# Batches of 3, 3 and 2 steps in the attention of an image network's first layer

## The chip, the cores and the metric

The kernel runs on one core of a Trainium2 chip, everything in fp32. The metric is the device time of one execution in microseconds (us). The kernel before takes 3935.89 us, the median of three runs (3935.14 to 3937.17).

## What is computed

Eight images of 512 channels and 32 x 32 positions go through four layers: attention with eight heads and three inner steps (layer 0), attention with one head of 512 channels (layer 1), an upsampling, leaky ReLU and downsampling (layer 2), and convolutions with mixed experts (layer 3). The change lies in layer 0, which is, cut to what matters:

```python
h = group_norm(x, gn_scale, gn_bias)
q, k, v = split(einsum('oc,bchw->bohw', qkv_w, h) + qkv_b)      # 8 heads of 64 channels
attn = softmax(einsum('bnsd,bntd->bnst', q, k) * 64 ** -0.5, axis=-1)   # 1024 x 1024 a head
h = einsum('bnst,bntd->bnsd', attn, v)
for _ in range(3):                                              # inner steps
    h = h + 0.1 * tanh(h @ inl_w.T + inl_b)
x = x + (proj_w @ h + proj_b)
```

## The kernel before, in words

`tile_sequence` works image by image: layer 0, layer 1, layer 2, and at the end layer 3 for all images. A second copy of the program, which subtracts row maxima before the exponentials, follows behind a condition and is not taken with these inputs.

In layer 0 the projections q, k and v of an image come first (`product`, L384: a matrix product in seven smaller ones, whose matmuls stand at L414). Then comes the attention of the image, the part that changes. It has eight **groups** (L596), one for each of four pairs of heads and each half of the 1024 queries, and each group has eight **steps**, one for each 128 keys: 64 steps an image, 512 in all.

- `scores(t)` (L599) makes one step's scores: two matmuls (L266), one for each head of the pair, each with a contraction over 64 rows, side by side in the array, into the two banks of one PSUM tile of pool `ps_sc`. ScalarE takes the exponential of both banks in one instruction (L612) into a buffer `e` of SBUF. VectorE adds `e` to the running sum of the group (L616, L618).
- `weighted(t)` (L620) multiplies the exponentials with the values (L627): two matmuls of 64 columns each, into one bank of pool `ps_mm` that gathers all eight steps of the group.
- `normalised(g)` (L632) ends a group: two matmuls with ones make the totals over the keys (L637) in a bank of pool `ps_tp`; VectorE takes their reciprocal (L641) and multiplies the gathered values with it into `hf` (L642); GpSimd adds the sums and the reciprocal to a guard that is looked at once at the end (L644).

A matmul of the program is two matmul instructions in the profile.

[...]`ps_sc` two tiles of two banks, `ps_tp` two banks, `ps_mm` two banks. Each pool hands out its buffers in turn, and a tile can be written once the tile that had the buffer before has been read. The exponentials have five buffers in turn (`tmp`, L77), the running sums two (L80).

The loop (L647) sets the order of TensorE: two steps of scores, then the values of the two steps before them, and so on. `normalised(g)` follows in the batch that holds steps 2 and 3 of the next group. The order of instructions is finally set by the framework's own scheduler, which may move an instruction ahead of others of its engine; in the attention it leaves TensorE in the order of the loop.

After the groups come the inner steps. The first one (L657 to L662) may begin before the last group is done: its first two products (P1 and C11 of `product`, written to `inl_A`) need only the first half of the positions. Their two banks are one of `ps_mm` and one of `ps_tp` (L661). The next product needs sums and differences of the four quarters of `hf` (`quarter_sums`, L365, with its subtractions at L378 to L381).

## Time and profile before

| what | us | share or count |
| --- | --- | --- |
| span of the profiled execution | 3934.4 | 37957 instructions |
| TensorE matmuls busy | 3868.2 | 98% |
| TensorE weight loads busy | 2032.6 | 52%, beside matmuls |
| VectorE busy | 2593.8 | 66% |
| ScalarE busy | 1105.0 | 28% |
| GpSimd busy | 436.1 | 11% |
| scores, L266, on the chain that ended last | | 13% of the span |
| values, L627, on the same chain | | 11% of the span |
| totals, L637 | 66.2 | 256 instructions |
| one image's attention, TensorE busy, from 564 to 691 us | 125.86 of 127.00 | 536 instructions |

An engine that is busy 98% of the span does not tell by itself that it sets the time; the chain of work that ended last, followed back from the end, does: 90% of it is TensorE. A group's line gives its count, the busy time of all its instructions together and the mean of one; the matmuls of a pair run side by side, so that the mean (616 ns for scores) is more than busy time over count. Behind the bar stands the idle time of the engine just before these instructions, and what ended it. In a timeline, equal instructions that follow each other are one row: its start, its length and their number.

### The profile page before, as it was taken

What the parts mean: (1) busy time and instruction counts of PE and PEld (TensorE: products, weight loads), DVE (VectorE), ACT (ScalarE), POOL (GpSimd) and SP (SyncE); (2) the same over time, 40 slices, a digit from 0 to 9 for tenths busy, and PEclk for the clock granted to TensorE, in tenths of its full rate; (3) what the DMA queues carried; (4) which work ended last, traced back from release to release, by engine and by line L of the source; (5) the groups of instructions that cost most, each with busy time, mean ns of one, the idle gap of its engine ahead of it and who ended that gap; (6) DMA issues with size and microseconds to landing.
All of it is one profiled execution on the core that took longest, in us unless ns stands there. A gap on an engine that the chain in (4) does not pass through costs nothing.

```text
span 3934.4 us, 37957 instructions
## 1 busy us (share of the span) xinstructions
PE 3868.2 (98%) x14630; PEld 2032.6 (52%) x14630; DVE 2593.8 (66%) x3690; ACT 1105.0 (28%) x1507; POOL 436.1 (11%) x310
## 2 busy tenths in 40 slices
PE   8999999999999999999999999999999999999998
PEld 4336653476435763366434754357534764346543
DVE  4777848764686647775586646765487655766786
ACT  1421224212332114212241123322142122421333
POOL 5310003000120003100030002200031001301000
PEclk9999999999999999999999999999999999999999
DMA  5002310122101310023101221013200131003432
GB/s 197 19 0 83 115 57 1 40 77 100 38 0 59 118 68 11 0 83 115 56 1 59 79 81 37 1 70 107 78 1 24 60 115 57 1 0 112 164 134 103
DMA packets 85792, 247.86 MB, mean 63 GB/s; under 512 B 10480, under 2 KB 33024, under 8 KB 78816
## 3 DMA queue, kind: packets, MB, share of 16 engines
q1 hardware_dynamic: 69712, 220.23, 15.8%
q10 hardware_dynamic: 13824, 12.59, 1.0%
q0 software_dynamic: 2064, 12.51, 0.8%
q8 instruction: 117, 1.92, 0.2%
q14 instruction: 75, 0.61, 0.0%
HBM read 185.40 MB, written 59.90 MB: 62 GB/s over the span
## 4 chain that ended last, share of the span: by engine, by line
PE 90%; DVE 7%; issue 1%; DMA 1%; ACT 1%; SPq 0%; DVEq 0%; ACTq 0%
PE scores L266 13%; PE av L627 11%; PE inl_X L414 6%; PE dn L941 6%; PE up L920 5%; PE v_X L414 4%; PE inl_Y L414 4%; PE av_X L854 4%; PE c L1150 3%; PE v_Y L414 3%; PE av_A L854 3%; PE v_A L414 3%; PE inl_A L414 3%; PE av_Y L854 2%; PE proj_X L414 2%; PE q_X L414 2%
## 5 line engine op out<-in xcount | busy, mean ns | idle before, releaser
L612 ACT ACTIVATE e<-scores 128x1024 f32<-128x1024 f32 x512 | 497.1, 1021 | 632.7 <-PE scores L266 632.0
L618 DVE TENSOR_TENSOR acc<-acc,e 128x1024 f32<-128x1024 f32 x384 | 494.1, 1287 | 122.7 <-ACT e L612 101.6
L266 PE MATMUL scores<-q,k 64*128 64x512 f32 x2048 | 511.0, 616 | 7.0 <-ACT e L612 3.6
L627 PE MATMUL av<-e,v 128*64 128x512 f32 x2048 | 494.1, 604 | 0.0
L644 POOL TENSOR_TENSOR seen<-seen,acc 128x512 f32<-128x512 f32 x128 | 212.3, 1659 | 1574.9 <-DVE acc L618 1569.9
L266 PEld LDWEIGHTS scores<-q,k 64*128 64x128 f32 x2048 | 175.7, 186 | 334.3 <-ACT e L612 163.2
L627 PEld LDWEIGHTS av<-e,v 128*64 128x64 f32 x2048 | 124.8, 136 | 338.8 <-issue 335.8
L941 PEld LDWEIGHTS dn<-dn_op,up 128*128 128x128 f32 (+1 forms) x2048 | 239.9, 192 | 46.3 <-issue 24.3
L904 DVE SCALAR_TENSOR_TENSOR up<-up,leak 128x512 f32<-128x512 f32 (+1 forms) x264 | 174.9, 687 | 132.9 <-ACT leak L903 124.9
L941 PE MATMUL dn<-dn_op,up 128*128 128x126 f32 (+5 forms) x2048 | 244.7, 275 | 10.1 <-DVE up L904 9.5
L903 ACT ACTIVATE leak<-up 128x512 f32<-128x512 f32 (+1 forms) x264 | 150.0, 595 | 248.9 <-DVE up L904 125.4
L641 DVE RECIPROCAL inv<-total 128x512 f32<-128x512 f32 x64 | 214.7, 3354 | 0.0
L920 PE MATMUL up<-halo,up_op 126*128 126x512 f32 (+1 forms) x384 | 182.8, 605 | 0.4 <-DVE up L904 0.3
L414 PE MATMUL inl_X<-T_hf,w_inl 128*128 128x512 f32 x384 | 172.6, 592 | 0.0
L644 POOL TENSOR_TENSOR seen<-seen,inv 128x512 f32<-128x512 f32 x64 | 125.1, 1955 | 417.6 <-DVE inv L641 417.6
L414 PE MATMUL inl_A<-hf,w_inl 128*128 128x512 f32 x384 | 169.5, 594 | 0.0
L616 DVE TENSOR_TENSOR acc<-e,e 128x1024 f32<-128x1024 f32 x64 | 85.0, 1329 | 102.4 <-ACT e L612 100.7
L508 ACT ACTIVATE inl_U<-inl_U,inl_b 128x512 f32<-128x512 f32 x96 | 64.0, 714 | 304.7 <-DVE inl_U L523 304.7
L519 DVE TENSOR_TENSOR inl_U<-inl_X,inl_P 128x512 f32<-128x512 f32 x96 | 61.8, 685 | 116.0 <-PE inl_X L414 116.0
L736 POOL TENSOR_TENSOR seen<-seen,acc 128x512 f32<-128x512 f32 x16 | 22.6, 1410 | 1019.9 <-DVE acc L728 1019.9
L1150 PE MATMUL c<-rim,mixed 128*128 128x512 f32 x288 | 124.9, 592 | 0.0
L414 PEld LDWEIGHTS inl_A<-hf,w_inl 128*128 128x128 f32 x384 | 72.3, 190 | 94.5 <-issue 88.8
(302 smaller groups left out, 5757.6 us busy)
## 6 DMA issues: line engine op xcount, KB each, us to landing
halo<-ypad_u SPq DMA_DIRECT2D x128, 252.0 KB
halo<-ypad_u SPq DMA_DIRECT2D x128, 198.0 KB
w_v<-stored_u_v SPq DMA_DIRECT2D x14, 1792.0 KB
x<-in_x_dram SPq DMA_DIRECT2D x32, 512.0 KB
spill_u<-z SPq DMA_DIRECT2D x28, 512.0 KB
z<-spill_u SPq DMA_DIRECT2D x28, 512.0 KB
out_dram<-z SPq DMA_DIRECT2D x28, 512.0 KB
w_q<-stored_u_q SPq DMA_DIRECT2D x7, 1792.0 KB
```

The lines of the kernel that those rows point to most:

```text
L266: nc.tensor.matmul(ps[r], k[r], q[r], start=True, stop=(shift is None))
L414: nc.tensor.matmul(dst, lhs, rhs, start=(opens and s == 0 and cc == 0), stop=(cc == 1 and s == rows), skip_group_check=True,)
L612: nc.scalar.activation(e, ps, AF.Exp, scale=HD ** -0.5)
L618: nc.vector.tensor_add(accs[g], accs[g], e)
L627: nc.tensor.matmul(avs[g][rows[r]], v[:, jc, ts(2 * oc + r, HD)], e[:, ts(r, HALF)], start=(jc == 0), stop=(jc == SC - 1),)
L641: nc.vector.reciprocal(inv, ps)
L644: nc.gpsimd.tensor_add(seen, seen, part)
L854: nc.tensor.matmul(ps[:, ts(s, QR)], left[:, j, at : at + P], right[:, j, :], start=(what in ("P1", "U2", "W") and s == 0 and j == 0), sto ...
L904: nc.vector.scalar_tensor_tensor(dst, ps, SQRT2, t, ALU.mult, ALU.max)
L920: nc.tensor.matmul(ps[i], op[0 : IR * n, :], halo.tile(t)[0 : IR * n, c + i, :], start=True, stop=True,)
L941: nc.tensor.matmul(rows[:, r0 - first : r1 + 1 - first, c0 : c1 + 1], up[t][0:k, c, ts(cc, P)], op[:, r0 - 4 * t + 3 : r1 + 4 - 4 * t, c0 ...
L1150: nc.tensor.matmul(banks[g].rearrange("p (h w) -> p h w", w=W), wt[:, at : at + P], h1[:, ky + 16 * g : ky + 16 * g + 16, kx : kx + W], st ...
```

## The change

Scores and values alternate in batches of three, three and two steps, so that a group has three batches instead of four. The first and second batches have three score steps that are all made before the values of the batch before. For the third one `ps_sc` has no buffer, so steps 2 and 5 of a group get two single banks of `ps_tp` instead, and two exponentials of 512 columns in place of one of 1024. Six steps' exponentials may be alive at once, so the buffers of exponentials become six. `normalised(g)` follows in the third batch of the next group, that is behind the values of its steps 3, 4 and 5; for the last group it follows at the end, as before. The purpose is that TensorE switches less often between the 64-row tiles of the scores and the 64-column tiles of the values.

```diff
         if n == HALF:
             return work.tile([P, n], F32, tag="half", name=name, bufs=2)
-        return work.tile([P, n], F32, tag="tmp", name=name, bufs=5)
+        return work.tile([P, n], F32, tag="tmp", name=name, bufs=6)
...
         def scores(t):
             g, jc = divmod(t, SC)
             oc, sh = groups[g]
-            ps = ps_sc.tile([P, S], F32, tag="scores", name=f"scores_{b}_{t}")
+            apart = jc in (2, 5)
+            if apart:
+                ps = [bank(ps_tp, f"scores_{b}_{t}_{r}") for r in range(2)]
+            else:
+                pair = ps_sc.tile([P, S], F32, tag="scores", name=f"scores_{b}_{t}")
+                ps = [pair[:, ts(r, HALF)] for r in range(2)]
             scores_T(
-                [ps[:, ts(r, HALF)] for r in range(2)],
+                ps,
...
             e = tmp(f"e_{b}_{t}", S)
-            nc.scalar.activation(e, ps, AF.Exp, scale=HD ** -0.5)
+            if apart:
+                for r in range(2):
+                    nc.scalar.activation(e[:, ts(r, HALF)], ps[r], AF.Exp, scale=HD ** -0.5)
+            else:
+                nc.scalar.activation(e, pair, AF.Exp, scale=HD ** -0.5)
...
-        n = len(groups) * SC
-        for t in range(0, n + 4, 2):
-            for u in (t, t + 1):
-                if u < n:
-                    scores(u)
-            for u in (t - 2, t - 1):
-                if 0 <= u < n:
-                    weighted(u)
-            if t >= SC + 2 and (t - 2) % SC == 0:
-                normalised((t - 2) // SC - 1)
+        batches = [
+            range(g * SC + i, g * SC + j)
+            for g in range(len(groups)) for i, j in ((0, 3), (3, 6), (6, 8))
+        ]
+        for i in range(len(batches) + 1):
+            for t in batches[i] if i < len(batches) else ():
+                scores(t)
+            for t in batches[i - 1] if i else ():
+                weighted(t)
+
+            g, part = divmod(i, 3)
+            if g and (part == 2 or i == len(batches)):
+                normalised(g - 1)
```

## The prediction, made before the changed kernel had run

> **What bounds the kernel now.** I read the page first: the busy shares, the chain that ended last, and the costliest groups.

> ```profile
> PE 3868.2 (98%) x14630; PEld 2032.6 (52%) x14630; DVE 2593.8 (66%) x3690; ACT 1105.0 (28%) x1507; POOL 436.1 (11%) x310
> ...
> PE 90%; DVE 7%; issue 1%; DMA 1%; ACT 1%; SPq 0%; DVEq 0%; ACTq 0%
> ...
> L612 ACT ACTIVATE e<-scores 128x1024 f32<-128x1024 f32 x512 | 497.1, 1021 | 632.7 <-PE scores L266 632.0
> L618 DVE TENSOR_TENSOR acc<-acc,e 128x1024 f32<-128x1024 f32 x384 | 494.1, 1287 | 122.7 <-ACT e L612 101.6
> L266 PE MATMUL scores<-q,k 64*128 64x512 f32 x2048 | 511.0, 616 | 7.0 <-ACT e L612 3.6
> L627 PE MATMUL av<-e,v 128*64 128x512 f32 x2048 | 494.1, 604 | 0.0
> ...
> L641 DVE RECIPROCAL inv<-total 128x512 f32<-128x512 f32 x64 | 214.7, 3354 | 0.0
> ```

> TensorE sets the time, and attention is 511.0 + 494.1 us of it. ScalarE waits for TensorE (632.0 us), while TensorE waits for ScalarE 3.6 us in the whole run. So only two things can move the time: what TensorE itself spends in attention, or a new wait on it. Next the timeline inside one attention (image 1; start, length, engine):

> ```profile
> 577.39 1.94 PE L627 MATMUL av<-e,v 128*64 128x512 f32 x8
> 579.26 1.99 PE L266 MATMUL scores<-q,k 64*128 64x512 f32 x8
> 581.18 1.94 PE L627 MATMUL av<-e,v 128*64 128x512 f32 x8
> 582.94 1.03 PE L637 MATMUL total<-acc,ones 128*64 128x512 f32 x4
> 583.90 1.99 PE L266 MATMUL scores<-q,k 64*128 64x512 f32 x8
> 584.02 3.36 DVE L641 RECIPROCAL inv<-total 128x512 f32<-128x512 f32 x1
> 587.52 2.06 POOL L644 TENSOR_TENSOR seen<-seen,inv 128x512 f32<-128x512 f32 x1 [8.21 <-DVE inv L641]
> ```

> Here: TensorE alternates without a gap. A block of two score steps starts 1.92 us before the values (579.26 to 581.18), a block of two value steps 1.87 us before the scores (577.39 to 579.26). The reciprocal begins 1.08 us after the totals begin, runs 3.36 us, and nothing on TensorE waits for it. Last, the timelines of the start and the end of the same attention:

> ```profile
> 560.48 1.13 PE L266 MATMUL scores<-q,k 64*128 64x512 f32 x4
> 562.03 1.13 PE L266 MATMUL scores<-q,k 64*128 64x512 f32 x4 [0.41 <-DVE v L495]
> 564.06 2.04 PE L266 MATMUL scores<-q,k 64*128 64x512 f32 x8 [0.91 <-ACT e L612]
> 566.04 1.94 PE L627 MATMUL av<-e,v 128*64 128x512 f32 x8
> ```

> ```profile
> 683.68 1.99 PE L266 MATMUL scores<-q,k 64*128 64x512 f32 x8
> 685.59 3.65 PE L627 MATMUL av<-e,v 128*64 128x512 f32 x16
> 690.32 1.08 PE L637 MATMUL total<-acc,ones 128*64 128x512 f32 x4 [1.07 <-DVE acc L618]
> 691.33 7.13 PE L414 MATMUL inl_A<-hf,w_inl 128*128 128x512 f32 x16
> 694.14 3.35 DVE L641 RECIPROCAL inv<-total 128x512 f32<-128x512 f32 x1
> 699.51 2.84 PE L414 MATMUL inl_X<-v,w_inl 128*128 128x512 f32 x6 [0.18 <-DVE v L379]
> ```

> At the start TensorE idles 0.41 + 0.91 us. At the end it idles 1.07 us for the last running sum, and then the inner step's first product (inl_A, 7.13 us) covers the last reciprocal.

> [...] Scores run in 64-row tiles, values and totals in 64-column tiles. [...] so a score matmul that waits for a bank holds everything behind it. The totals' wait above is such a case. [...] A third pair of scores therefore needs two more banks, and the change takes the only two that `ps_tp` has.

> **The change, part by part.**

> *Fewer switches.* Sixteen value matmuls take 3.65 us and eight take 1.94, so two steps stream in 1.71 us; for scores x8 less x4 gives 0.86 us a step. A block of two score steps costs 1.92 - 1.72 = 0.20 us over streaming, a block of two value steps 1.87 - 1.71 = 0.16. One alternation costs 0.35 us. A group of 8 steps has 4 alternations now and 3 after: 64 groups x 0.35 = **-22.4 us**. Totals follow values in the same tiling and cost the same as before.

> *The two half exponentials for steps 2 and 5.* The trace of layer 1 has such halves at 0.5 us apiece, so a step takes 1.03 instead of 1.02 us of ScalarE, which waits for TensorE anyway: 0. *The sixth buffer.* Three steps in work and three being made are 6; the exponential of step t waits for the addition of step t-6, which is done at least a block before: 0.

> *Totals two batches later, in the same pool as steps 2 and 5.* This is the added wait. `ps_tp` hands out two banks in turn. A group now takes five: step 2's pair, step 5's pair, the total. The next pair takes the other bank first and the total's own bank second, and that one is free only when the reciprocal has read it. The built order of instructions says so: the second matmul of step 2 of the next group waits for VectorE, at the count of that reciprocal; its first matmul waits for nothing. Queued behind it on TensorE are two value steps, and everything else. With the totals starting at 0: the score block starts at 0.96 (583.90 - 582.94); its third step would start at 0.96 + 0.10 (half of the block's switch cost) + 2 x 0.86 = 2.78. The reciprocal starts at 1.08, if VectorE is free, and ends at 1.08 + 3.36 = 4.44. VectorE is free: the addition of the last exponential, made before three value steps and the totals, ends about 0.8 us before. A release takes 0.06 us (the last addition ended 690.26, the totals that waited for it began 690.32), and weights not loaded ahead cost 0.05 to 0.10 us. So the matmul runs at 4.60 instead of 2.78: a stall of 1.82 us. It comes after groups 0 to 5 of an image; total 6 is followed by values, total 7 by the inner step. 6 x 8 images = 48 stalls x 1.82 = **+87.4 us**. Bounds: 1.55 (weights loaded ahead, an early release) to 2.0 (an addition still running before the reciprocal): 74 to 96 us.

> *The start.* Steps 0 to 5 come before the first values. Step 2 has banks at once and fills the 0.91 us idle; steps 3, 4 and 5 then follow the exponentials of 0, 1 and 2, at 1.02 us each, slower than streaming. I put the first values at about 567.1 with six steps done, against 566.04 with four; two steps are worth 1.72, so -0.65 us an image: **-5 us** (-2 to -8).

> *The end.* Total 6 now comes just before total 7 and its reciprocal just before the last. The inner step's first product writes into a bank that the sixth group's values held, freed only by that group's multiplication, which the order puts behind both reciprocals (about 13.0 us after the start of the last score block). The order meets this by doing the other bank's half first, both its products. Counted from that score block: totals 7 end at 8.0, the first half waits for reciprocal 6 until 9.0, its second product about 0.9 for a copy, the other half starts at 13.5 and finds its bank free. The waiting product of the sums starts at 18.0; before, it started at 699.51 - 683.68 = 15.83, with a value step and a total (1.72 us) less to do. So 18.0 - 17.55 = +0.5 us an image: **+4 us** (0 to +10). The 1.07 us that total 7 waits for now is in this.

> Sum: -22.4 + 87.4 - 5 + 4 = +64 us; 3935.9 + 64 = 4000 us.

> **Rivals.** *The wait is hidden* (7%): were the bank free earlier than the count of the reciprocal says, the switches alone would show: 3935.9 - 22.4 - 5 + 4 = 3912 us, faster. The order of instructions speaks against it; for it only that the wait is not in the trace of before, so that its length is worked out and not seen. *The pair is torn wholly apart* (5%): if the first matmul of the waiting pair is held as well and the two then run one after the other, each stall grows by one matmul, 0.86 us: 48 x 0.86 = 41, 4041 us. The score pairs start within 0.01 us of each other in the trace, so they do depend on issue order. *The end goes wrong* (5%): VectorE's three subtractions took up to 1.75 us beside GpSimd in the trace of before, 0.68 alone; if the four that stand behind the last multiplication all take that, the product of the sums slips by some 4 us an image: +32, 4032 us. *VectorE becomes the bound* (1%): it has 7 x 1.29 + 3.36 + 0.68 = 13.1 us of work in a group of 15.6 to 17.5 us.

> **How the numbers follow.** The likeliest case (82%) gives 4000 us. Its unknown terms, 74 to 96 for the stalls, -2 to -8 and 0 to +10 at the ends, span 3980 to 4020. Below lies the hidden wait, above the other two. A result within 0.2% of no change would need the stalls to come to just 23 us: 1%. Faster 7%, slower 92%.

> **What would show it.** In the profile after: groups of 15.65 us become 17.5 (totals to totals, 16.00 now); a line in which scores wait some 1.8 us, 48 times, for the reciprocal; alternations of 0.35 us, three in a group; the reciprocal still 1.08 us behind its totals. It would be wrong if scores wait for nothing or for ScalarE, or if the reciprocal starts late.

## The result, and the profile after

| | us, median | from | to |
| --- | --- | --- | --- |
| before | 3936.53 | 3935.14 | 3940.61 |
| after | 4006.66 | 4004.24 | 4008.63 |

The changed kernel takes 1.0176 times as long (95% interval 1.0159 to 1.0194): 70 us more, where 64 were forecast. The page of the changed kernel, busy times, the engines of the chain that ended last, and the costliest groups:

```profile
PE 3905.6 (97%) x14630; PEld 2062.1 (51%) x14630; DVE 2660.6 (66%) x3690; ACT 1109.9 (28%) x1635; POOL 425.6 (11%) x310
...
PE 91%; DVE 7%; DMA 1%; ACT 1%; issue 0%; SPq 0%; POOL 0%; ACTq 0%; POOLq 0%; DVEq 0%
...
L627 DVE TENSOR_TENSOR acc<-acc,e 128x1024 f32<-128x1024 f32 x384 | 537.1, 1399 | 121.3 <-ACT e L621 93.2
L266 PE MATMUL scores<-q,k 64*128 64x512 f32 x2048 | 548.5, 612 | 37.0 <-DVE inv L650 33.2
...
L636 PE MATMUL av<-e,v 128*64 128x512 f32 x2048 | 481.4, 601 | 0.0
...
L650 DVE RECIPROCAL inv<-total 128x512 f32<-128x512 f32 x64 | 213.7, 3350 | 46.6 <-PE total L646 46.6
...
L619 ACT ACTIVATE e<-scores 128x512 f32<-128x512 f32 x256 | 145.7, 610 | 52.1 <-PE scores L266 52.1
```

TensorE still sets the time, and ScalarE still waits for it. The new thing stands behind the bar of the scores' line (L266): 33.2 us of idle time that the reciprocal ended. The scores are also busy 37.5 us longer (511.0 before), though their 2048 matmuls are the same; the values (L636) are busy 12.7 us less (494.1 before). The waits of TensorE (engine line, engine line waited for, us in total, times, longest us) count the new ones:

```profile
PE scores L266 <- DVE inv L650: 33.2, 48, 0.7
...
PE inl_A L414 <- DVE inv L650: 7.1, 8, 0.9
PE inl_A L414 <- ACT inl_P L514: 5.4, 8, 0.7
```

There are 48 waits of scores for the reciprocal, as many as forecast, but at 0.69 us each and not at 1.8. The timeline of one group, from its totals on, tells why; its columns are start, length, engine, line:

```profile
598.01 1.03 PE L646 MATMUL total<-acc,ones 128*64 128x512 f32 x4
...
598.97 2.84 PE L266 MATMUL scores<-q,k 64*128 64x512 f32 x10
599.09 3.36 DVE L650 RECIPROCAL inv<-total 128x512 f32<-128x512 f32 x1 [0.83 <-PE total L646]
...
602.50 1.12 PE L266 MATMUL scores<-q,k 64*128 64x512 f32 x2 [0.69 <-DVE inv L650]
...
603.55 1.94 PE L636 MATMUL av<-e,v 128*64 128x512 f32 x8
...
615.46 1.03 PE L646 MATMUL total<-acc,ones 128*64 128x512 f32 x4
```

The score block has twelve matmul instructions, and ten of them run from 598.97. Eight belong to steps 0 and 1, two to the waiting pair: its first matmul has its bank, and both its instructions run alone, at 2.78 and 3.21 us after the totals began. Its second one needs the bank of the total. The reciprocal starts 1.08 us after the totals (599.09 - 598.01) and ends at 4.44; the last two instructions run from 4.49, and the values behind them on TensorE from 5.54. So TensorE counts as busy while only one of the two halves of the array works, and is wholly idle for 0.69 us only. What the wait costs is read from the period, from totals to totals. It is 17.45 us after each of the groups 0 to 5 of an image (here 615.46 - 598.01). Before it was 16.00: in the trace before, the totals at 582.94 are followed by these.

```profile
598.94 1.03 PE L637 MATMUL total<-acc,ones 128*64 128x512 f32 x4
```

With one alternation less the period would be 15.65, as two experiments below confirm. So the stall is 17.45 - 15.65 = **1.80 us**, and 48 of them are 86 us.

The end of the same attention:

```profile
698.19 1.99 PE L266 MATMUL scores<-q,k 64*128 64x512 f32 x8
...
702.73 1.03 PE L646 MATMUL total<-acc,ones 128*64 128x512 f32 x4
...
703.59 1.89 PE L636 MATMUL av<-e,v 128*64 128x512 f32 x8
...
703.81 6.57 DVE L650 RECIPROCAL inv<-total 128x512 f32<-128x512 f32 x2 [0.83 <-PE total L646]
...
705.31 1.03 PE L646 MATMUL total<-acc,ones 128*64 128x512 f32 x4
...
707.22 1.98 PE L414 MATMUL inl_A<-hf,w_inl 128*128 128x512 f32 x4 [0.89 <-DVE inv L650]
...
716.08 2.74 PE L414 MATMUL inl_X<-v,w_inl 128*128 128x512 f32 x6
```

The waiting product of the sums starts 716.08 - 698.19 = 17.89 us after the last score block. Before it was 15.83, with 1.72 us less to do: +0.34 us an image.

Added up over the attention of an image, from the first matmul of its q to the first one of `inl_Y` in both traces, the change costs 7.69 and 7.52 us in the first two images and 8.18 to 8.20 in the six others: **64.4 us** together. The two profiled spans differ by 71.4 us (4005.8 and 3934.4). The other 7 lie outside the attention, above all in layer 2, where stretches of the trace after show TensorE at half its clock. The table by window of one of them (us of the window, PE, PEld, DVE, ACT and POOL busy, granted clock as a share of full speed, share of the DMA engines, GB/s):

```profile
2300.00:2304.00 4.00, 2.44 (x18) 1.87 (x16) 0.90 (x3) 0.79 (x2) 0.00 (x0) 1.00 0.69 218
2304.20:2311.00 6.80, 6.41 (x30) 6.42 (x31) 1.62 (x3) 1.31 (x4) 0.00 (x0) 0.50 0.79 254
2311.00:2316.00 5.00, 5.00 (x47) 5.00 (x46) 0.00 (x0) 0.98 (x2) 0.00 (x0) 1.00 0.87 281
```

The clock falls to 0.50 after TensorE waited in the stretch before, and 6.8 us later it is back. All such stretches together are 34.5 us after and 21.3 before, and TensorE is busy in 20.15 and 9.30 us of them. With half of that put down as lost, an estimate from the granted 0.50, it is 10.1 against 4.7, some 5.4 us. The change does not bring this wait with it. The same one stands in the trace before, where no half clock follows:

```profile
2260.00:2264.00 4.00, 2.18 (x17) 1.83 (x15) 1.33 (x3) 1.09 (x2) 0.00 (x0) 1.00 0.74 234
2264.00:2268.00 4.00, 3.90 (x35) 3.90 (x35) 1.34 (x3) 1.62 (x3) 0.00 (x0) 1.00 0.77 245
```

The last section sets the two side by side. How much of the 5.4 us the timed runs lost too is open. The unchanged kernel itself varies so: in 36 further runs of it the mean granted clock lay between 0.995 and 0.998 and the time between 3949 and 3935 us. The run of it that was profiled, at 0.998, was among those with the least half clock.

### The profile page after: what moved, and what is told of

It is laid out like the page before. It is cut to its first block, busy times and chain, and to the rows that moved or that the text cites. A ratio compares the mean times of both kernels' runs of the same rounds, so it can differ in the third digit from the quotient of the medians.

```text
span 4005.8 us, 37999 instructions
## 1 busy us (share of the span) xinstructions
PE 3905.6 (97%) x14630; PEld 2062.1 (51%) x14630; DVE 2660.6 (66%) x3690; ACT 1109.9 (28%) x1635; POOL 425.6 (11%) x310
## 3 DMA queue, kind: packets, MB, share of 16 engines
q8 instruction: 117, 1.92, 0.2%
## 4 chain that ended last, share of the span: by engine, by line
PE 91%; DVE 7%; DMA 1%; ACT 1%; issue 0%; SPq 0%; POOL 0%; ACTq 0%; POOLq 0%; DVEq 0%
PE av L636 11%; PE scores L266 11%; PE inl_X L414 6%; PE dn L954 6%; DVE inv L650 5%; PE up L933 5%; PE v_X L414 4%; PE inl_A L414 4%; PE inl_Y L414 4%; PE av_X L867 4%; PE c L1163 3%; PE v_Y L414 3%; PE av_A L867 3%; PE v_A L414 3%; PE av_Y L867 2%; PE proj_X L414 2%
## 5 line engine op out<-in xcount | busy, mean ns | idle before, releaser
L627 DVE TENSOR_TENSOR acc<-acc,e 128x1024 f32<-128x1024 f32 x384 | 537.1, 1399 | 121.3 <-ACT e L621 93.2
L266 PE MATMUL scores<-q,k 64*128 64x512 f32 x2048 | 548.5, 612 | 37.0 <-DVE inv L650 33.2
L621 ACT ACTIVATE e<-scores 128x1024 f32<-128x1024 f32 x384 | 372.8, 1024 | 480.7 <-PE scores L266 480.6
L636 PE MATMUL av<-e,v 128*64 128x512 f32 x2048 | 481.4, 601 | 0.0
L266 PEld LDWEIGHTS scores<-q,k 64*128 64x128 f32 x2048 | 195.4, 186 | 383.2 <-issue 280.2
L653 POOL TENSOR_TENSOR seen<-seen,acc 128x512 f32<-128x512 f32 x128 | 245.3, 1916 | 1356.5 <-DVE acc L627 1347.1
L636 PEld LDWEIGHTS av<-e,v 128*64 128x64 f32 x2048 | 130.6, 136 | 326.8 <-issue 307.8
L414 PE MATMUL inl_A<-hf,w_inl 128*128 128x512 f32 x384 | 173.7, 598 | 12.5 <-DVE inv L650 7.1
L414 PE MATMUL inl_X<-T_hf,w_inl 128*128 128x512 f32 x384 | 172.6, 592 | 0.0
L619 ACT ACTIVATE e<-scores 128x512 f32<-128x512 f32 x256 | 145.7, 610 | 52.1 <-PE scores L266 52.1
L653 POOL TENSOR_TENSOR seen<-seen,inv 128x512 f32<-128x512 f32 x64 | 81.2, 1268 | 694.8 <-DVE inv L650 694.2
L625 DVE TENSOR_TENSOR acc<-e,e 128x1024 f32<-128x1024 f32 x64 | 110.6, 1728 | 47.3 <-ACT e L621 47.3
L749 POOL TENSOR_TENSOR seen<-seen,acc 128x512 f32<-128x512 f32 x16 | 22.8, 1428 | 1041.6 <-DVE acc L741 1041.6
L414 PEld LDWEIGHTS inl_A<-hf,w_inl 128*128 128x128 f32 x384 | 71.0, 190 | 111.7 <-issue 74.6
```

What stands on the lines that cost most here:

```text
L266: nc.tensor.matmul(ps[r], k[r], q[r], start=True, stop=(shift is None))
L414: nc.tensor.matmul(dst, lhs, rhs, start=(opens and s == 0 and cc == 0), stop=(cc == 1 and s == rows), skip_group_check=True,)
L621: nc.scalar.activation(e, pair, AF.Exp, scale=HD ** -0.5)
L627: nc.vector.tensor_add(accs[g], accs[g], e)
L636: nc.tensor.matmul(avs[g][rows[r]], v[:, jc, ts(2 * oc + r, HD)], e[:, ts(r, HALF)], start=(jc == 0), stop=(jc == SC - 1),)
L653: nc.gpsimd.tensor_add(seen, seen, part)
```

## The experiments

The theory: a pair of scores waits until the reciprocal has read the total's bank, because the totals now come just ahead of the next pair from the same pool (1.80 us, 48 times), and fewer alternations save 0.35 us each. Rivals: the third score step itself, its half exponentials or the sixth buffer slow the attention; or the totals are costly because they come late, bank or no bank.

**Totals one batch earlier.** The totals go behind the batch of values before; batches, banks and buffers stay.

```diff
-            if g and (part == 2 or i == len(batches)):
+            if g and (part == 1 or i == len(batches)):
```

> The changed kernel with one word altered: a group's totals follow in the second batch of the next group (part == 1), one batch earlier than in the change. The next pair of single banks is then wanted not 2.78 us after the totals begin but about 7.4 us after (two more score steps, three value steps), and the reciprocal has let go at 4.5. Theory of the bank held by the reciprocal: no wait of scores for VectorE, groups of 15.65 us from totals to totals; per image 8 alternations x 0.35 = -2.8 us, -0.1 at the start, about -1.2 at the end (the wait of the last totals for the last sum, 1.07 us, is covered): -4.1 x 8 = -33 us, so about 3903 us. Rival, that batches of three or the split exponentials are slow in themselves (VectorE or ScalarE late): groups stay near 17.4 us and the time near 4000 us.

Measured: 3917.14 us (3914.61 to 3920.33), 0.9942 of before (0.9925 to 0.9959); a second time, in other runs, 3916.19 us and 0.9932 (0.9916 to 0.9949).

> e1 unchanged, beside e5 on the same chip: -23 us against the kernel before, as the profile of e1 gave it in the attentions alone (-2.8 us an image, -3.3 in the first two).

One number turns +70 us into -22, and the second time into -27. The group in the timeline:

```profile
659.47 1.03 PE L646 MATMUL total<-acc,ones 128*64 128x512 f32 x4
...
660.43 1.99 PE L266 MATMUL scores<-q,k 64*128 64x512 f32 x8
660.54 3.36 DVE L650 RECIPROCAL inv<-total 128x512 f32<-128x512 f32 x1 [0.30 <-PE total L646]
...
662.34 2.79 PE L636 MATMUL av<-e,v 128*64 128x512 f32 x12
...
665.07 2.85 PE L266 MATMUL scores<-q,k 64*128 64x512 f32 x12
...
675.11 1.03 PE L646 MATMUL total<-acc,ones 128*64 128x512 f32 x4
...
677.01 3.35 DVE L650 RECIPROCAL inv<-total 128x512 f32<-128x512 f32 x1
...
683.70 1.08 PE L646 MATMUL total<-acc,ones 128*64 128x512 f32 x4 [1.20 <-DVE acc L627]
```

After the totals now comes a block of two score steps, which needs no bank of that pool. The block of three comes 5.60 us after the totals, when the reciprocal is done, and its twelve instructions are one unbroken row. From totals to totals: 675.11 - 659.47 = 15.64 us. So the third step, the half exponentials and the sixth buffer cost nothing that shows, and three alternations save what was forecast. Of the 14 us that I missed 3.5 are the kernel before itself, whose median in these runs was 3939.45, and some 10 are at the end: I expected the wait of 1.07 us for the last running sum to go, and it is 1.20 us now. The reciprocal of group 6 (677.01 to 680.36) is in VectorE's queue ahead of the last additions. An image gains 3.26, 3.44 and six times 2.77 us in its attention, 23.3 in all.

**The bank freed by a copy.** The changed kernel with the totals where they are, but copied out of their bank by ScalarE; VectorE takes the reciprocal of the copy.

```diff
-            nc.vector.reciprocal(inv, ps)
+            nc.scalar.copy(inv, ps)
+            nc.vector.reciprocal(inv, inv)
```

> The changed kernel, but ScalarE first copies the totals out of their bank (about 0.6 us) and VectorE takes the reciprocal of the copy in SBUF. The totals stay where the change put them. Theory: the bank is free about 1.8 us after the totals begin, before the next pair wants it at 2.78, so the 48 waits vanish and the groups take 15.65 us; the end stays about as in the changed kernel (+0.3 to +1 us an image): (-2.8 - 0.1 + 0.8) x 8 = -17 us, about 3920 us. Rival, that the late place of the totals costs by itself (VectorE's order, values waiting for the bank of an older group): groups stay near 17.4 us, time near 4000 us.

Measured: 3931.71 us (3927.98 to 3934.32), 0.9975 of before (0.9965 to 0.9985).

```profile
604.01 1.03 PE L646 MATMUL total<-acc,ones 128*64 128x512 f32 x4
...
604.97 2.85 PE L266 MATMUL scores<-q,k 64*128 64x512 f32 x12
605.08 0.59 ACT L650 COPY inv<-total 128x512 f32<-128x512 f32 x1 [2.50 <-PE total L646]
...
605.70 3.35 DVE L651 RECIPROCAL inv<-inv 128x512 f32<-128x512 f32 x1
...
607.74 1.94 PE L636 MATMUL av<-e,v 128*64 128x512 f32 x8
```

The bank is free 1.66 us after the totals began, ahead of the 2.78 at which it is wanted. The twelve score instructions run through, though the totals come as late as in the changed kernel, and each group takes 15.65 us. This tells the bank from the lateness. The time is 12 us above what I expected. Of these, 3.5 are again the kernel before (3939.45), and some 5.5 are the end, which I had put about as long as in the changed kernel: copy and reciprocal follow each other where nothing hides them, and the way from the last totals to the product of the sums is 1.16 us an image longer than there, 9.3 us in all. The attention gains 11.5 us where 17 were expected; the remaining 3 us lie outside it.

**Batches of two in the new form.** The changed kernel (single banks for steps 2 and 5, half exponentials, six buffers, late totals), with the batches of the kernel before.

```diff
-            for g in range(len(groups)) for i, j in ((0, 3), (3, 6), (6, 8))
+            for g in range(len(groups)) for i, j in ((0, 2), (2, 4), (4, 6), (6, 8))
...
-            g, part = divmod(i, 3)
-            if g and (part == 2 or i == len(batches)):
+            g, part = divmod(i, 4)
+            if g and (part == 3 or i == len(batches)):
```

> The changed kernel with batches of two steps (four to a group): steps 2 and 5 still in single banks with split exponentials, six buffers, totals in the last batch of the next group, where the next pair is wanted about 4.85 us after them. Theory: no wait worth naming, alternations as in the kernel before, so groups of 16.00 us and a total within 4 us of 3936 us. Against e1, what is left is the price of the alternations alone: 0.35 us for each, one more in a group. Rival, that the split into single banks and halves of exponentials is what costs: groups above 16.5 us.

Measured: 3943.6 us (3939.19 to 3950.26), 1.0011 of before (1.0002 to 1.002). Groups take 16.00 us, as before: there is no stall, because here the totals are followed by a block that holds steps 0 and 1 only. All that the change adds beside the batches costs an image +0.02, -0.16 and six times +0.51 us, 2.9 in all, and that at the ends.

**Batches of one.** The same with batches of a single step: eight alternations a group instead of four.

```diff
-            for g in range(len(groups)) for i, j in ((0, 3), (3, 6), (6, 8))
+            for g in range(len(groups)) for i, j in [(s, s + 1) for s in range(SC)]
...
-            g, part = divmod(i, 3)
-            if g and (part == 2 or i == len(batches)):
+            g, part = divmod(i, 8)
+            if g and (part == 5 or i == len(batches)):
```

> The changed kernel with batches of one step, eight alternations a group, totals behind the fifth step of the next group. Theory, one alternation costs 0.35 us whatever the size of the batches: a group takes 13.73 + 0.86 + 8 x 0.35 = 17.4 us, an image 11.3 us more than before, 4026 us in all, with no wait on TensorE. Rival, that an alternation is cheaper when batches are short (part of the 0.35 is weights not loaded ahead): groups nearer to 16.7.

Measured: 4040.62 us, 1.0251 of before (1.023 to 1.0271).

```profile
603.27 1.13 PE L266 MATMUL scores<-q,k 64*128 64x512 f32 x4
...
604.33 1.08 PE L636 MATMUL av<-e,v 128*64 128x512 f32 x4
...
605.34 1.13 PE L266 MATMUL scores<-q,k 64*128 64x512 f32 x4
```

One step, scores and values, takes 605.34 - 603.27 = 2.07 us; its streaming is 0.86 + 0.855 = 1.715, so the alternation is 0.35 us. No wait of the scores is in it, and a group takes 17.40 us, which is 1.40 more than 16.00: four more alternations at 0.35. From blocks of two to blocks of three it is 16.00 - 15.65 = 0.35 again, so the price does not depend on the length of the blocks. The rest (12.34 us an image in most of them, where 8 x 1.40 is 11.2) is at start and end.

**The late totals alone, in the kernel before.**

```diff
-        for t in range(0, n + 4, 2):
+        for t in range(0, n + 8, 2):
...
-            if t >= SC + 2 and (t - 2) % SC == 0:
-                normalised((t - 2) // SC - 1)
+            if t >= SC + 6 and (t - 6) % SC == 0:
+                normalised((t - 6) // SC - 1)
```

> The kernel before, with batches of two, five buffers and no scores in the single banks; only the totals follow two batches later. Theory: no score wants the totals' bank, so the groups stay at 16.00 us; at the end of an image the inner step's first product waits for banks as in the changed kernel, while the wait of the last totals (1.07 us) goes: about +0.1 us an image, 3937 us in all. Rival, that late totals cost the time: groups near 17.4 us, about 4000 us.

Measured: 3945.83 us (3941.89 to 3953.19), 1.0016 of before (1.0009 to 1.0022). Groups stay at 16.00 us. The timeline of the end has the 6 us:

```profile
689.98 6.56 DVE L641 RECIPROCAL inv<-total 128x512 f32<-128x512 f32 x2
...
693.39 1.98 PE L414 MATMUL inl_A<-hf,w_inl 128*128 128x512 f32 x4 [1.40 <-DVE inv L641]
...
696.05 3.70 PE L414 MATMUL inl_A<-hf,w_inl 128*128 128x512 f32 x8 [0.68 <-ACT inl_P L514]
```

Two reciprocals in a row hold back the inner step's first product by 1.40 us, and a copy by another 0.68, against waits of 1.07 and 0.18 us before. Over the attention that is 0.77 us an image, 6.1 in eight, where I expected 0.1 an image. The late totals do cost something, then, but only at the end, and a tenth of what the change lost.

**The bank held longer.** The changed kernel, with a copy on VectorE ahead of the reciprocal, whose result is overwritten: the bank comes free one copy later, and nothing else changes.

```diff
+            nc.vector.tensor_copy(inv, ps)
             nc.vector.reciprocal(inv, ps)
```

> The changed kernel with one more instruction of VectorE: it copies the totals out of their bank (about 0.7 us, overwritten at once) before the reciprocal reads the same bank. Theory: the bank is let go about 0.7 to 0.8 us later, and each of the 48 waits grows by as much: groups of 18.2 us in place of 17.45, at the end of an image about 1 us more; 48 x 0.75 + 8 = +44, about 4050 us. Rival, that the wait is for something else that happens to end with the reciprocal: groups stay at 17.45.

Measured: 4096.71 us, 1.0393 of before (1.0372 to 1.0414). First a group in the timeline, then the table by window of this and of another group, and of two stretches within this one (TensorE alone; us, PE busy, granted clock, DMA share, GB/s):

```profile
609.34 1.03 PE L646 MATMUL total<-acc,ones 128*64 128x512 f32 x4
...
610.30 2.84 PE L266 MATMUL scores<-q,k 64*128 64x512 f32 x10
610.41 0.69 DVE L650 COPY inv<-total 128x512 f32<-128x512 f32 x1 [0.83 <-PE total L646]
...
611.14 3.36 DVE L651 RECIPROCAL inv<-total 128x512 f32<-128x512 f32 x1
...
614.64 1.55 PE L266 MATMUL scores<-q,k 64*128 64x512 f32 x2 [1.51 <-DVE inv L651]
```

```profile
609.34:629.23 19.89, 18.38 (x71) 0.91 0.00 0
669.05:687.29 18.24, 16.73 (x70) 1.00 0.00 1
...
611.73:615.15 3.42, 1.91 (x8) 1.00 0.00 0
615.15:618.56 3.41, 3.41 (x8) 0.50 0.00 0
```

In 17 of 48 groups the period is 18.24 us, 0.79 more than 17.45, as expected: the bank is released at 5.16 us after the totals instead of 4.44, and the stall follows the release. In the other 31 it is 19.89, and in exactly these a stretch of 3.41 us at half clock begins 5.8 to 7.3 us after the totals; half of 3.41 is 1.7, and 19.89 - 18.24 = 1.65. So the groups cost 17 x 0.79 + 31 x 2.44 = 89 us more than in the changed kernel, where I expected 36; the half clock was not in my sum. In the timed runs it is 153 us over the kernel before of the same runs (3943.58), against 70 for the changed kernel: 83 more.

**Threes throughout.** The two parts that worked, the longer blocks and the copy, with batches of three that run on over the borders of groups: 22 alternations an image instead of 24 (32 before). The totals follow earlier, at once behind the block of values that holds a group's last step.

```diff
-            apart = jc in (2, 5)
+            apart = t % 3 == 2
...
-            nc.vector.reciprocal(inv, ps)
+            nc.scalar.copy(inv, ps)
+            nc.vector.reciprocal(inv, inv)
...
-        batches = [
-            range(g * SC + i, g * SC + j)
-            for g in range(len(groups)) for i, j in ((0, 3), (3, 6), (6, 8))
-        ]
+        batches = [range(i, min(i + 3, len(groups) * SC)) for i in range(0, len(groups) * SC, 3)]
...
-            g, part = divmod(i, 3)
-            if g and (part == 2 or i == len(batches)):
-                normalised(g - 1)
+            for t in batches[i - 1] if i else ():
+                if t % SC == SC - 1:
+                    normalised(t // SC)
```

> Batches of three steps throughout, across the borders of the groups (22 batches an image in place of 24 in the change and 32 before); the third step of each batch in the single banks; ScalarE copies the totals out of their bank as in e2; a group's totals follow directly behind the values of its last step. Theory: the copy frees the bank about 1.8 us after the totals begin, before the next third step wants it at 2.78; 10 alternations fewer than before, 10 x 0.35 = -3.5 us an image, -0.1 at the start, about 0 at the end: -29 us, about 3910 us, some 6 us less than e1. Rival, that VectorE (13.1 us in a group of 15.3 us) or the six buffers bind now: no faster than e1.

Measured: 3908.68 us (3902.45 to 3912.3), 0.9911 of before (0.9894 to 0.9927), the fastest of all, and 7.5 us less than the totals one batch earlier took in the same runs (3916.19). Its page:

```profile
L266 PE MATMUL scores<-q,k 64*128 64x512 f32 x2048 | 490.7, 609 | 3.8 <-DVE v L495 3.3
```

No score waits for a reciprocal or an exponential; the 3.3 us of waiting for v at the start were there before. Ten alternations fewer at 0.35 are 3.5 us an image, 28 in all; the attention gains 34.6, the rest at the ends. Blocks, copy and place of the totals change together here; the run does not say what each of them gives.

## Why the prediction was right

- **Fewer switches, -22.4 us.** Right. Groups without the stall take 15.65 us against 16.00 in two experiments, and the batches of one give the same 0.35 us from the other side. So these runs put 0.35 us on a change there and back. In the trace after, the first pair of matmuls of a block takes 0.69 us (scores) or 0.64 us (values) and a later one 0.59, which is 0.15 of the 0.35; the weights of a first pair are loaded only as it starts (598.97 for both), those of a later pair 0.43 us ahead. The other 0.20 stands between the blocks: there a pair starts 0.53 us after the one before it, twice in an alternation, and inside a block 0.43. What TensorE does in that time the trace does not show.
- **Half exponentials and sixth buffer, 0.** Right in the sum. A half takes 0.57 us of ScalarE (145.7 over 256), not the 0.5 of layer 1, so that a step of two halves takes 1.14. TensorE does not wait for it; the first experiment shows both parts in place without a cost.
- **The stall, 1.82 us x 48 = +87.4.** Measured 1.80 x 48 = 86. The reciprocal started at the forecast 1.08 and ended at the forecast 4.44. The rival "torn wholly apart" put one more matmul on top, 41 us; in fact the first matmul of the waiting pair ran early and alone, and only the second came behind the reciprocal, with its two instructions at 4.49 and 5.02 and the values at 5.54. I had put its start at 4.60: the release was quicker, but the two instructions then took 1.05 us instead of 0.86 and the switch, so that the stall came out within 0.02.
- **The start, -5 us.** Missed: -0.67 and -0.75 in the first two images, as forecast, but -0.09 in the other six, some -2 in all. The forecast took the 0.91 us for which TensorE waits in image 1 for all eight images. In six of them that wait is 0.30 us in the trace before, and there was less to fill. (The 3.6 us of the scores' line are just these waits, 2 x 0.91 + 6 x 0.30.) Images 0 and 1 wait longer since ScalarE loads the table of the exponential, 1.28 us, right before the first exponential (at 561.69 in image 1); in the six others it has done so 22 us before the first scores.
- **The end, +4 us.** Right in kind, the reciprocal of group 6 ahead of the last one and the first product waiting for it; about +0.3 us an image, so +2 to +3.
- **The sum, +64 us.** The attention gives 64.4. That it is so close is in part luck: the start gave 3 us less than forecast, the end and the stalls cost 1 to 2 and 1 us less. The 70 us of the timed runs have 6 more. In the profiled run such a rest lies outside the attention, for the most part in stretches of half clock. That term was not in my sum, and the range took it in without my having thought of it.
- **"A line in which scores wait some 1.8 us, 48 times."** The count was right, the length in that line was not: 0.69 us. What I had forecast is the loss of the period; the line shows only the time in which no part of TensorE worked, for the pair was torn: one of its matmuls ran early.
- **The rivals.** The wait was not hidden; the end did not slip by 4 us; VectorE was free at each reciprocal that scores wait for (0.83 us idle before it).

Three experiments settle the cause. With the same blocks of three, the stall goes when the bank is wanted later (totals one batch earlier) and when it is released earlier (totals as late, but copied out in 0.59 us), and it grows by 0.79 us when the bank is released 0.72 us later.

## What to carry to other kernels

When two users share a pool of buffers, ask in which order they take them, and how long each holds its own: here a bank was wanted 2.78 us after the totals began, and its reader, a reciprocal of 3.36 us, let it go at 4.44; where the totals stand in the loop decided between +70 and -22 us. Price a stall by the period of the loop and not by the idle time that a line shows: 33 us of idle time were 86 us of loss, since a torn pair keeps half the array busy. A slow reader of a shared bank can be taken off it by a short copy on an engine that has time, but where nothing hides the copy, as at the end of an image here, it costs time. The kernel with the copy was 8 us faster than the kernel before; the one with the totals moved was 22 us faster and needed no further instruction.

## What was not expected of the hardware

The length of the wait does not tell the 31 from the 17. What the traces show besides is where the stretches at 0.50 begin: before, at 426.69, 3628.39 and 3928.76 us; after, at 433.68, 2304.18, 3696.82 and 4000.60. Within each of these two traces they are whole multiples of 3.4133 us from one another, to 0.02 us (938 and 88; 548, 408 and 89). Measured in lengths of 3.41 us that end where such a stretch can begin, the waits differ in where they fall. In the group at 609.34 above, one length, 611.73 to 615.15, holds the whole wait of 1.51 us, and the half clock begins at its end. The two waits in layer 2 differ in the same way: after, one length, 2300.77 to 2304.18, holds 1.74 us of idle time, and the half clock begins at its end; before, the idle time is cut into 1.03 us (2259.65 to 2263.06) and 0.89 us (2263.06 to 2266.47), and none follows. That this tells the 31 from the 17 as well is my reading, which no run tests.

Idle time in one length does not settle it alone. The 1.51 us in the kernel that holds the bank longer brought the half clock; in the trace after, 1.70 us near the end (3993.78 to 3997.19) did not. What makes the difference is not shown. A wait that brings the half clock costs twice: in the kernel that holds the bank longer, 0.79 us more for the wait itself and 1.65 for the clock.
